# Spreading layer-1 products over the blocks of a GATv2/GCN kernel, and a new order for its end

## Chip, core, metric

The kernel runs on one core of a Trainium2 chip. The metric is device microseconds of one execution; runs are compared by their median.

## What is computed

Two graph layers over 3327 nodes (padded to 3328 = 26 blocks of 128) with 128 features and a sparse adjacency matrix (about 2% of the entries are not zero). Layer 0 is a four-head GATv2, layer 1 a normalised graph convolution. Both are pre-norm with a residual:

```python
h = jnp.maximum(_layernorm(x, axis=-1), 0.0)
# layer 0, for each head
x1 = h @ w1; x2 = h @ w2
E = leaky_relu(x1[:, None, :] + x2[None, :, :], 0.01)
s = jnp.exp(jnp.tanh((E @ a) / 8.0) * 8.0) * adj
s = s / jnp.sum(s, axis=-1, keepdims=True)
out_h = leaky_relu(s @ h @ Wlin.T, 0.01)
x = x + concat(out_h) @ w
# layer 1
h = jnp.maximum(_layernorm(x, axis=-1), 0.0)
A_t = adj + I;  D = A_t.sum(axis=1);  A_norm = D**-0.5 * A_t * D**-0.5
x = x + relu(A_norm @ (h @ W.T + b))
```

## The kernel before

**Layer 0, block by block.** A block is 128 rows of the adjacency matrix. For each block the kernel finds the columns of the non-zero entries, builds lists of row numbers from them, and fetches those rows of two feature tables in DRAM with indirect DMAs that POOL issues (`gather`, line 562). A block has two halves; a half has four windows of 8 gathers (tile `g`, four buffers) and an overflow window of 3 (tile `ge`, one buffer): 70 gathers a block, 1820 in all. TensorE turns the rows (`stage_z`, L587), DVE applies the maximum with the block's own term (L599), TensorE sums to scores (`stage_r`, L610), `finish` makes weights of them and sums the weighted rows (`ag`, L658 and L676), and `close` completes the block: it writes the new x to DRAM (`xn_d`), and leaves in `x_sb[:, b]` the normalised, projected and scaled row block that layer 1 multiplies (L749). A block whose `x_sb` is final is called closed.

**Order.** The schedule is written out by hand. A score group is a slot pair; `slot()` advances everything that runs beside the groups: the closing chains (`tails`), the chains of `finish` (`ends`), the preparation of coming blocks (`advance`, 72 steps a block, some 108 slots a block), and the gathers that fit. Each engine runs its own instructions in this order.

**Preparation** (`prep(b)`) runs a block or more ahead. It turns the 26 column tiles of the block with TensorE, copies them to SBUF tiles `at` (pool `pat`, 3 buffers) with ACT, and writes them to DRAM (`AT_d`, from ACT's queue). `AT_d` holds the transposed matrix by strips: strip s is the four blocks 4s to 4s+3 (the seventh strip has two), so `AT_d` tile (s, j) is 128x512. Then come the list steps: `hTb` is loaded (L424), ACT sums the rows (L426), the next block's `adjb` is loaded (L342, SP's queue, one buffer), the sorted lists are made, and the indices (L450).

**Layer 1** is, for each strip s, a sum over j of `x_sb[:, j]` times tile (s, j), 26 x 7 products, most 128x512. They are made in several places:

- in preparation, from the `at` tiles still in SBUF, for the columns j below `finished(b)` = 4*(b//4) - 2: `known_step` (L370), summed in `part1`, stored to `part1_d` (72 tile columns of a strip in all).
- in the last block and a half, when preparation is over: `begin` (L873), for strips 1 to 3, twelve columns each from `finished(4s)`; tiles come in pairs from `AT_d` to the room of `adjb`, the sum goes to `part2_d`.
- at the end: `layer1` (L937), 74 products. Tiles come 11 at a time into the `g` buffers (`strip`, L847, SP's and ACT's queues). The work begins with strips 0 and 1 without the last column (36 products, one in each slot while the last block's chain runs), then goes strip by strip. `strip_in` loads x, `part1` and, for strips 1 to 3, `part2` (SP's queue, L892 to L896) into two pairs of buffers `r0`, `r1`. `strip_out` adds them, turns the result, scales it, applies relu and the residual and writes the output (L917, ACT's queue).

The half of a table that depends on the adjacency matrix is rewritten for each half block (`weights`, L572, SP's queue).

Of the kernel before, what the change touches and what calls it, by code (L numbers as in the profile page):

```python
# [15 lines left out]
P = 128  # L16
# [3 lines left out]
BANK = 512  # L20
# [44 lines left out]
COLS = 709  # L65
FEAT = 64
# [162 lines left out]
def _sparse_layers(tc, nc, x, adj, w1, w2, a, wlin, w, gw, gb, gb_sb, gwT, x_sb, dinv, flag, ident, out):  # L229
# [24 lines left out]
    with ExitStack() as l0:  # L254
# [26 lines left out]
        pat = l0.enter_context(tc.tile_pool(name="pat", bufs=3))  # L281
# [62 lines left out]
        def prep(b, k):  # L344
# [21 lines left out]
            def known_step(j0, js, at):  # L366
                assert all(blks[j0 + q].closed for q in js)
                pq = bank()
                for q in js:
                    nc.tensor.matmul(pq[:, :P], x_sb[:, j0 + q, :], at[:, q, :], start=(q == 0), stop=(q == js[-1]))  # L370
                yield
                if j0 == 0:
                    k.part1 = pb.tile([P, P], F32, name="part1")
                    nc.scalar.copy(k.part1, pq[:, :P])
                else:
                    nc.vector.tensor_add(k.part1, k.part1, pq[:, :P])
                if j0 + len(js) == finished(b):
                    nc.sync.dma_start(part1_d[:, b * P:(b + 1) * P], k.part1)
# [47 lines left out]
            nc.scalar.activation(adjb, adjb, AF.Copy, accum_out=deg)  # L426
            if 0 < b < NB - 1:
                load(b + 1)
# [23 lines left out]
            k.idx = idx  # L452
            yield
            flat = cand[:, :, :SOME]
# [92 lines left out]
        def rows_in():  # L547
            state["turn"] += 1
            return pgs[state["turn"] % 4].tile([P, WT, ROW], F32, name="g")

        def gather(b, hb, w):

            k = blks[b]
            tab = tables[hb].rearrange("r (c u) -> (r c) u", u=1)
            if w == NW:
                g, n, at = pe_.tile([P, OVT, ROW], F32, name="ge"), OVT, k.idxo[:, hb]
            else:
                g, n, at = rows_in(), WT, k.idx[:, w, WT * hb:WT * hb + WT]

            def one(t):  # L560
                lo = 16 * (t // 2) if w < NW else 0
                return nc.gpsimd.indirect_dma_start(out=g[:, t, lo:COLS], out_offset=None, in_=tab,  # L562
                                                    in_offset=bass.IndirectOffsetOnAxis(ap=at[:, t:t + 1], axis=0))

            queue.extend((k, hb, w, partial(one, t)) for t in range(n))
            k.g[hb, w] = g
# [47 lines left out]
        def finish(k, hb, w):  # L614
# [4 lines left out]
            if w < NW:  # L619
                wq = pb.tile([P, WT, 8], F32, name="wq")  # L620
                diag = bass.AP(g.tensor, g.offset, [list(g.ap[0]), [ROW + 8, 8], [1, 8]])
                nc.vector.tensor_tensor(wq, diag, qmask[:, None, :].to_broadcast([P, WT, 8]), OP.mult)
# [203 lines left out]
        BEGUN = 12  # L826
        strips = {}
        early = {s: range(finished(4 * s), finished(4 * s) + BEGUN) for s in (1, 2, 3) if finished(4 * s) + BEGUN < NB - 3}
# [22 lines left out]
        def begin():  # L851
# [17 lines left out]
            for i, (s, j) in enumerate(work):  # L869
                assert blks[j].closed  # L870
                if j == early[s][0]:
                    po = bank()
                nc.tensor.matmul(po, x_sb[:, j, :], thirds[:, i // PAIR % 3, i % PAIR], start=(j == early[s][0]), stop=(j == early[s][-1]))  # L873
                if i % PAIR == PAIR - 1:
                    bring(i // PAIR + 3)
                if j == early[s][-1]:
                    part2 = pv.tile([P, H, P], F32, name="outT").rearrange("p h i -> p (h i)")
                    nc.scalar.copy(part2, po)
                    nc.sync.dma_start(part2_d[:, 4 * s * P:4 * s * P + BANK], part2)
# [3 lines left out]
        def first_column(s):  # L883
            return early[s][-1] + 1 if s in early else finished(4 * s)

        def strip_in(s):
# [8 lines left out]
            if s in early:  # L895
                nc.sync.dma_start(r0[:, 1], part2_d[:, rows].rearrange("p (b i) -> p b i", b=n))  # L896
            return n, rows, r0, r1

        def strip_out(s, po, n, rows, r0, r1):
# [3 lines left out]
            if s in early:  # L903
                nc.vector.tensor_add(ot, po, ot)
            if finished(4 * s):
                nc.vector.tensor_add(ot, ot if s in early else po, r1[:, 0])
            elif s not in early:
# [12 lines left out]
        front = range(min(2, NS - 1))  # L920
        work = [(s, j) for s in front for j in range(first_column(s), NB - 1)]
        in_front = len(work)
        work += [(s, NB - 1) for s in front] + [(s, j) for s in range(len(front), NS) for j in range(first_column(s), NB)]
        pieces = [work[i:i + PIECE] for i in range(0, len(work), PIECE)]

        def layer1():
            ending, sums, ins = [], {}, {}
            for i, (s, j) in enumerate(work):
# [3 lines left out]
                if s not in sums:  # L932
                    sums[s] = ps_z.tile([P, 2, BANK], F32, name="z")[:, 0]
                if j == min(NB - 1, first_column(s) + 4 * (s not in front)):
                    assert len(ending) < 2
                    ins[s] = strip_in(s)
                nc.tensor.matmul(sums[s][:, :w], x_sb[:, j, :], strips[s, j][:, :w], start=(j == first_column(s)), stop=(j == NB - 1))  # L937
                if i % PIECE == PIECE - 1 or i == len(work) - 1:
                    allow("g")
                ending[:] = [f for f in ending if next(f, "end") != "end"]  # L940
                if j == NB - 1:
                    ending.append(strip_out(s, sums.pop(s), *ins.pop(s)))
                yield "one"
# [7 lines left out]
        with tc.tile_pool(name="pre", bufs=1) as pre, ExitStack() as images:  # L951

            lent = pe_.tile([P, OVT, ROW], F32, name="ge").rearrange("p t c -> p (t c)")[:, :16 * P]
# [353 lines left out]
```

## Time and profile before

| | |
|---|---|
| median of 3 runs | 3246.03 us (3227.53 to 3260.07) |
| the profiled execution | 2536.74 us; its span 2534.9 us, granted TensorE clock 0.98 |
| PE, DVE, POOL, ACT busy | 2278.9, 2030.5, 1791.8, 704.1 us |
| DMA | 838.58 MB, 331 GB/s over the span |
| of it: POOL's queue (gathers) | 640.34 MB |
| SP's queue, ACT's queue | 140.96 MB, 53.88 MB |
| HBM | 765.93 MB read, 113.42 MB written |

The profile is of one execution, which was shorter than the runs of the median; nothing in it says why. "Busy" counts an engine's instructions, not its waits; PE's ends are modelled. A row of windows gives a stretch in us, its length, the busy time (and number of instructions) of PE, its weight loads (PEld), DVE, ACT and POOL, then the granted clock, the share of time in which DMA engines had packets, and GB/s. A row of the timeline gives start, duration, engine, line, operation, tiles and, in brackets, the idle time before and what ended it. A row of waits gives who waited for whom: us in total, times, the longest.

### The profile page before, as it was taken

What the parts mean: (1) busy time and instruction counts of PE and PEld (TensorE: products, weight loads), DVE (VectorE), ACT (ScalarE), POOL (GpSimd) and SP (SyncE); (2) the same over time, 40 slices, a digit from 0 to 9 for tenths busy, and PEclk for the clock granted to TensorE, in tenths of its full rate; (3) what the DMA queues carried; (4) which work ended last, traced back from release to release, by engine and by line L of the source; (5) the groups of instructions that cost most, each with busy time, mean ns of one, the idle gap of its engine ahead of it and who ended that gap; (6) DMA issues with size and microseconds to landing.
All of it is one profiled execution on the core that took longest, in us unless ns stands there. A gap on an engine that the chain in (4) does not pass through costs nothing.

```text
span 2534.9 us, 51974 instructions
## 1 busy us (share of the span) xinstructions
PE 2278.9 (90%) x19410; PEld 1586.2 (63%) x19410; DVE 2030.5 (80%) x6260; ACT 704.1 (28%) x1651; POOL 1791.8 (71%) x1873
## 2 busy tenths in 40 slices
PE   6689899988989998989998999999999899999898
PEld 4456666656666666666666666666666667675553
DVE  7678988888788888878888788988988888895433
ACT  4122233223223222322322322232232233222110
POOL 3577777777777777777777777777777777777620
PEclk9789999999999999999999999999999999999999
DMA  9999999999999999999999999999999999999995
GB/s 294 392 338 314 342 353 318 334 351 335 324 339 346 318 328 359 329 319 343 337 312 336 353 311 341 352 329 329 339 346 318 330 360 313 333 322 347 324 336 186
DMA packets 460759, 838.58 MB, mean 331 GB/s; under 512 B 209099, under 2 KB 318165, under 8 KB 457173
## 3 DMA queue, kind: packets, MB, share of 16 engines
q0 software_dynamic: 145600, 640.34, 71.0%
q1 hardware_dynamic: 219396, 140.96, 19.1%
q10 hardware_dynamic: 95504, 53.88, 7.0%
q8 instruction: 156, 2.56, 0.4%
q14 instruction: 103, 0.84, 0.1%
HBM read 765.93 MB, written 113.42 MB: 347 GB/s over the span
## 4 chain that ended last, share of the span: by engine, by line
PE 35%; DVE 24%; DMA 20%; POOL 11%; issue 7%; ACT 1%; SPq 0%; DVEq 0%; POOLq 0%; ACTq 0%
DMA g<-table,idx 13%; DVE r L599 11%; POOL g L562 10%; PE z L587 10%; PE s L610 6%; PE z L590 3%; DMA ge<-table,idxo 3%; PE z L937 2%; DVE cand L405 2%; PE tr L627 2%; PE ag L658 2%; DMA AT_d<-at 2%; PE tr L370 2%; PE tr L505 1%; DVE codes L401 1%
## 5 line engine op out<-in xcount | busy, mean ns | idle before, releaser
L562 POOL DMA_INDIRECT g<-table,idx x1664 | 1616.3, 971 | 568.3 <-issue 442.2
L599 DVE TENSOR_TENSOR r<-z,x1n 128x1024 f32<-128x1024 f32 x832 | 1010.1, 1215 | 65.5 <-PE z L587 63.9
L587 PE MATMUL z<-ident,g 128*128 128x128 f32 x6656 | 922.4, 278 | 151.9 <-DVE r L599 111.7
L587 PEld LDWEIGHTS z<-ident,g 128*128 128x128 f32 x6656 | 743.8, 142 | 366.9 <-DVE r L599 224.2
L610 PE MATMUL s<-r,sel 128*32 128x512 f32 (+1 forms) x3744 | 491.1, 597 | 0.7 <-ACT ssb L618 0.7
L618 ACT COPY ssb<-s 128x512 f32<-128x512 f32 x260 | 146.7, 564 | 524.6 <-PE s L610 522.5
L630 DVE TENSOR_TENSOR sc<-tr,g 128x32 f32<-128x32 f32 x208 | 38.5, 185 | 300.5 <-PE tr L627 300.5
L405 DVE MAX8 cand<-codes 128x8 f32<-128x52 uint16 x1664 | 215.3, 205 | 0.0
L562 POOL DMA_INDIRECT ge<-table,idxo x156 | 152.6, 978 | 47.5 <-issue 38.1
L638 ACT ACTIVATE th<-sc 128x32 f32<-128x32 f32 x260 | 58.3, 224 | 420.9 <-DVE sc L633 418.5
L590 PE MATMUL z<-oi,x1b 128*128 128x384 f32 x416 | 174.1, 501 | 0.0
L658 PEld LDWEIGHTS ag<-g,wt 128*32 128x32 f32 x3328 | 99.0, 110 | 115.3 <-issue 100.8
L357 ACT COPY at<-tr 128x512 f32<-128x512 f32 (+1 forms) x175 | 97.0, 554 | 222.2 <-PE tr L355 198.3
L627 PE MATMUL tr<-ident,ssb 128*128 128x128 f32 x988 | 153.1, 276 | 5.0 <-ACT ssb L618 4.5
L610 PEld LDWEIGHTS s<-r,sel 128*32 128x32 f32 x3744 | 73.9, 108 | 110.5 <-issue 86.4
L587 PEld LDWEIGHTS z<-ident,ge 128*128 128x128 f32 x624 | 81.4, 146 | 94.8 <-issue 28.5
L596 ACT ACTIVATE r<-z 128x768 f32<-128x768 f32 x104 | 84.3, 810 | 201.7 <-PE z L590 201.7
L658 PE MATMUL ag<-g,wt 128*32 128x133 f32 x3328 | 133.4, 278 | 0.0
L587 PE MATMUL z<-ident,ge 128*128 128x128 f32 x624 | 111.7, 283 | 21.1 <-DMA ge<-table,idxo 18.5
L627 PEld LDWEIGHTS tr<-ident,ssb 128*128 128x128 f32 x988 | 114.3, 141 | 15.3 <-ACT ssb L618 14.9
L355 PE MATMUL tr<-ident,adjb 128*128 128x128 f32 x676 | 107.4, 282 | 16.3 <-DMA adjb<-in_adj_dram 10.2
L401 DVE SCALAR_TENSOR_TENSOR codes<-adjb,code 128x832 uint16<-128x832 f32 x104 | 102.3, 1020 | 1.9 <-DMA adjb<-in_adj_dram 1.9
(188 smaller groups left out, 2350.4 us busy)
## 6 DMA issues: line engine op xcount, KB each, us to landing
adjb<-in_adj_dram SPq DMA_DIRECT2D x26, 1664.0 KB
table<-AT_d SPq DMA_DIRECT2D x52, 832.0 KB
AT_d<-at ACTq DMA_DIRECT2D x150, 256.0 KB
g<-table,idx POOLq DMA_INDIRECT x1664
table<-img SPq DMA_DIRECT2D x12, 1312.0 KB
adjb<-AT_d SPq DMA_DIRECT2D x18, 512.0 KB
g<-AT_d SPq DMA_DIRECT2D x7, 1024.0 KB
g<-AT_d ACTq DMA_DIRECT2D x5, 1024.0 KB
```

Source lines behind the costliest of these rows:

```text
L355: nc.tensor.transpose(pt[:, q, :], adjb[:, (j0 + q) * P:(j0 + q + 1) * P], ident)
L357: nc.scalar.copy(at[:, :n, :], pt[:, :n, :])
L401: nc.vector.scalar_tensor_tensor(codes[:, i], adjb[:, c0:c0 + part], 0.0, code[:, c0:c0 + part], op0=OP.not_equal, op1=OP.mult, accum_out= ...
L405: nc.vector.max(cand[:, c, 8:].rearrange("p (r s) -> p r s", s=32)[:, :, sgm % 32], codes.rearrange("p a b -> p (a b)")[:, sgm % 32 * SEG: ...
L562: return nc.gpsimd.indirect_dma_start(out=g[:, t, lo:COLS], out_offset=None, in_=tab, in_offset=bass.IndirectOffsetOnAxis(ap=at[:, t:t + 1 ...
L587: nc.tensor.matmul(z[:, i, q * P:(q + 1) * P], g[:, m % 2 * 4 + q, PROJ + h * D:PROJ + (h + 1) * D], ident, is_transpose=True, start=(q == ...
L590: nc.tensor.matmul(z[:, i, :n], k.x1b[:, h * D:(h + 1) * D], k.oi[:, hb * n:(hb + 1) * n], start=False, stop=True, skip_group_check=True)
L599: nc.vector.tensor_tensor(r.rearrange("p h (i s) -> p h i s", s=16), z.rearrange("p h (i s) -> p h i s", s=16), k.x1n[:, 2 * hp:2 * hp + 2 ...
L610: nc.tensor.matmul(k.s[32 * h:32 * h + 32, :n], sel[:, h, 31 - at:63 - at], rs[h // 2][:, h % 2, :n], start=(at == 0), stop=(at == 1 or m ...
L618: nc.scalar.copy(ssb[:, :nk * P], s[:, :nk * P])
L627: nc.tensor.transpose(pt[:, q, :], ssb[:, q * P:(q + 1) * P], ident)
L658: nc.tensor.matmul(ag[32 * cg:32 * cg + 32, u, :WORK], wt[:, t].rearrange("p h q -> p (h q)"), g[:, t, FEAT:FEAT + WORK], start=(w == 0 an ...
```

## The change

Preparation of block b may now take a run of three products of layer 1 (`part_of`). It picks the closed strip with the most columns that are ready (block closed, two behind) and not yet summed, loads three `AT_d` tiles from DRAM into the `at` buffers, and, if the strip has a sum already, that too (`part2_d`). The loads are issued after ACT's row sum and ahead of the next `adjb`; the six matmuls stand behind the index step; the sum is added (or copied, the first time) a step later and stored. `pat` has 4 buffers instead of 3; `part1` has one instead of two, and rows of `g` and `ge` are 712 wide instead of 720.

`begin` now takes four columns each of strips 0 to 5, from where the runs ended, and adds to the stored sum where there is one. `first_column` follows. In the end, the order is: strips 0 to 3 without the last column (12 products, in the slots of the last chain), then the last columns two at a time between the remaining strips: 29 products. Two strips share a double PSUM tile, and `strip_in` looks five products ahead.

```diff
+WIDE = 712
-        pat = l0.enter_context(tc.tile_pool(name="pat", bufs=3))
+        pat = l0.enter_context(tc.tile_pool(name="pat", bufs=4))
...
-                    k.part1 = pb.tile([P, P], F32, name="part1")
+                    k.part1 = pb.tile([P, P], F32, name="part1", bufs=1)
...
             nc.scalar.activation(adjb, adjb, AF.Copy, accum_out=deg)
+            mine = part_of(b)
+            next(mine)
             if 0 < b < NB - 1:
                 load(b + 1)
...
             k.idx = idx
-            yield
+            next(mine, None)
+            yield
+            next(mine, None)
...
-            return pgs[state["turn"] % 4].tile([P, WT, ROW], F32, name="g")
+            return pgs[state["turn"] % 4].tile([P, WT, WIDE], F32, name="g")
...
-                g, n, at = pe_.tile([P, OVT, ROW], F32, name="ge"), OVT, k.idxo[:, hb]
+                g, n, at = pe_.tile([P, OVT, WIDE], F32, name="ge"), OVT, k.idxo[:, hb]
...
-        BEGUN = 12
+        BEGUN = 4
+        RUN = 3
         strips = {}
-        early = {s: range(finished(4 * s), finished(4 * s) + BEGUN) for s in (1, 2, 3) if finished(4 * s) + BEGUN < NB - 3}
+        runs, known = {}, [finished(4 * s) for s in range(NS)]
+        for b in range(NB):
+            s = max(range(max(1, (b + 1) // 4)), key=lambda s: b - 2 - known[s])
+            if b >= 3 and b - 2 - known[s] >= RUN:
+                runs[b] = s, known[s]
+                known[s] += RUN
+        early = {s: range(known[s], known[s] + BEGUN) for s in range(NS - 1) if NB > 12 and known[s] + BEGUN < NB - 2}
+        begun = {s for s, _ in runs.values()}
+
+        def part_of(b):
+
+            if b not in runs:
+                yield
+                return
+            s, j0 = runs[b]
+            wide = AT_d[s * NP + j0 * P:s * NP + (j0 + RUN) * P, :].rearrange("(j p) i -> p j i", p=P)
+            cols = [pat.tile([P, 4, P], F32, name="at").rearrange("p a b -> p (a b)") for _ in range(RUN)]
+            for q in range(RUN):
+                nc.sync.dma_start(cols[q], wide[:, q])
+            total = pat.tile([P, 4, P], F32, name="at").rearrange("p a b -> p (a b)")
+            place = part2_d[:, 4 * s * P:4 * s * P + BANK]
+            if j0 > finished(4 * s):
+                nc.sync.dma_start(total, place)
+            yield
+            pq = bank()
+            for q in range(RUN):
+                assert blks[j0 + q].closed
+                nc.tensor.matmul(pq, x_sb[:, j0 + q, :], cols[q], start=(q == 0), stop=(q == RUN - 1))
+            yield
+            if j0 > finished(4 * s):
+                nc.vector.tensor_add(total, total, pq)
+            else:
+                nc.scalar.copy(total, pq)
+            nc.sync.dma_start(place, total)
...
+                place = part2_d[:, 4 * s * P:4 * s * P + BANK]
                 if j == early[s][0]:
                     po = bank()
+                    part2 = pat.tile([P, 4, P], F32, name="at").rearrange("p a b -> p (a b)")
+                    if s in begun:
+                        nc.sync.dma_start(part2, place)
...
                 if j == early[s][-1]:
-                    part2 = pv.tile([P, H, P], F32, name="outT").rearrange("p h i -> p (h i)")
-                    nc.scalar.copy(part2, po)
-                    nc.sync.dma_start(part2_d[:, 4 * s * P:4 * s * P + BANK], part2)
+                    if s in begun:
+                        nc.vector.tensor_add(part2, part2, po)
+                    else:
+                        nc.scalar.copy(part2, po)
+                    nc.sync.dma_start(place, part2)
...
-            return early[s][-1] + 1 if s in early else finished(4 * s)
+            return early[s][-1] + 1 if s in early else known[s]
...
-            if s in early:
+            if s in early or s in begun:
                 nc.sync.dma_start(r0[:, 1], part2_d[:, rows].rearrange("p (b i) -> p b i", b=n))
...
-        front = range(min(2, NS - 1))
-        work = [(s, j) for s in front for j in range(first_column(s), NB - 1)]
-        in_front = len(work)
-        work += [(s, NB - 1) for s in front] + [(s, j) for s in range(len(front), NS) for j in range(first_column(s), NB)]
+        left = [[(s, j) for j in range(first_column(s), NB)] for s in range(NS)]
+        if NS > 6:
+            rest, last = [part[:-1] for part in left], [part[-1:] for part in left]
+            order = rest[:4] + last[:2] + rest[4:5] + last[2:4] + rest[5:6] + last[4:6] + left[6:]
+            in_front = sum(map(len, rest[:4]))
+        else:
+            order, in_front = left, len(left[0]) - 1
+        work = [w for part in order for w in part]
...
                 if s not in sums:
-                    sums[s] = ps_z.tile([P, 2, BANK], F32, name="z")[:, 0]
-                if j == min(NB - 1, first_column(s) + 4 * (s not in front)):
-                    assert len(ending) < 2
-                    ins[s] = strip_in(s)
+                    if not banks:
+                        two = ps_z.tile([P, 2, BANK], F32, name="z")
+                        banks += [two[:, 0], two[:, 1]]
+                    sums[s] = banks.pop(0)
...
+                if i >= in_front - 1:
+                    for s1, j1 in work[i:i + 5]:
+                        if j1 == NB - 1 and s1 not in ins and s1 not in gone and len(ins) + len(ending) < 2 and (i >= in_front or s1 < NS - 3 or s1 == 0):
+                            ins[s1] = strip_in(s1)
                 ending[:] = [f for f in ending if next(f, "end") != "end"]
                 if j == NB - 1:
+                    if s not in ins:
+                        bring(s)
+                    gone.add(s)
                     ending.append(strip_out(s, sums.pop(s), *ins.pop(s)))
+                    next(ending[-1])
```

More of the change, by code (lines that the diff above doesn't have):

```diff
@@ L620, in finish @@
                 wq = pb.tile([P, WT, 8], F32, name="wq")
-                diag = bass.AP(g.tensor, g.offset, [list(g.ap[0]), [ROW + 8, 8], [1, 8]])
+                diag = bass.AP(g.tensor, g.offset, [list(g.ap[0]), [WIDE + 8, 8], [1, 8]])
                 nc.vector.tensor_tensor(wq, diag, qmask[:, None, :].to_broadcast([P, WT, 8]), OP.mult)
@@ L902, in strip_out @@
             po = po[:, :n * P].rearrange("p (b i) -> p b i", b=n)
-            if s in early:
+            more = s in early or s in begun
+            if more:
                 nc.vector.tensor_add(ot, po, ot)
             if finished(4 * s):
-                nc.vector.tensor_add(ot, ot if s in early else po, r1[:, 0])
-            elif s not in early:
+                nc.vector.tensor_add(ot, ot if more else po, r1[:, 0])
+            elif not more:
                 nc.scalar.copy(ot, po)
@@ L917, in strip_out, with bring @@
             nc.scalar.dma_start(out[rows, :].rearrange("(b p) d -> p b d", p=P), xo)
-        front = range(min(2, NS - 1))
-        work = [(s, j) for s in front for j in range(first_column(s), NB - 1)]
-        in_front = len(work)
-        work += [(s, NB - 1) for s in front] + [(s, j) for s in range(len(front), NS) for j in range(first_column(s), NB)]
+        left = [[(s, j) for j in range(first_column(s), NB)] for s in range(NS)]
[6 more added lines that the diff above has]
+        work = [w for part in order for w in part]
         pieces = [work[i:i + PIECE] for i in range(0, len(work), PIECE)]
         def layer1():
-            ending, sums, ins = [], {}, {}
+            ending, sums, ins, banks, gone = [], {}, {}, [], set()
+            def bring(s):
+                while len(ins) + len(ending) > 1:
+                    ending[:] = [f for f in ending if next(f, "end") != "end"]
+                ins[s] = strip_in(s)
             for i, (s, j) in enumerate(work):
@@ L951, in _sparse_layers @@
         with tc.tile_pool(name="pre", bufs=1) as pre, ExitStack() as images:
-            lent = pe_.tile([P, OVT, ROW], F32, name="ge").rearrange("p t c -> p (t c)")[:, :16 * P]
+            lent = pe_.tile([P, OVT, WIDE], F32, name="ge").rearrange("p t c -> p (t c)")[:, :16 * P]
             blks[0].at = list(lent.rearrange("p (i k c) -> p i k c", i=4, k=4)[:, i] for i in range(4))
```

## Prediction

> **What bounds the kernel now.** I read the page first: PE 90% busy, DVE 80%, POOL 71%, DMA engines near 9 in every slice. Busy shares don't say who sets the pace, so I went on to POOL's timeline inside the loop, where it only issues row gathers, and to windows of the gathers alone.
>
> ```profile
> L562 POOL DMA_INDIRECT g<-table,idx x1664 | 1616.3, 971 | 568.3 <-issue 442.2
> ...
> 1485.20 0.94 POOL L562 DMA_INDIRECT g<-table,idx  x1 [0.30 <-issue]
> 1486.45 0.95 POOL L562 DMA_INDIRECT g<-table,idx  x1 [0.30 <-issue]
> 1487.70 0.95 POOL L562 DMA_INDIRECT g<-table,idx  x1 [0.30 <-issue]
> ...
> 170.00:2427.00 2257.00, 1700.14 (x1751) 0.99 0.99 334
> ```
>
> Each gather takes 0.95 us and the next begins 0.30 us later with nothing awaited: one per 1.25 us. In 170 to 2427 us, 1751 gathers in 2257 us are 1.29 us each; a block has 70 of them, so 90 us. The 29% by which POOL looks idle is mostly this 0.30 us (1751 x 0.30 = 525 of 557 us). POOL's wait for a buffer that PE has still to read is small, the third row below. So in the loop POOL sets the pace. How near PE comes is read from windows of six blocks (548 to 1087) and four late ones (1540 to 1894), and from what PE waited for in the latter:
>
> ```profile
> 548.00:1087.00 539.00, 486.44 (x4346) 342.67 (x4347) 454.88 (x1404) 156.74 (x372) 409.72 (x421) 1.00 0.99 335
> 1540.00:1894.00 354.00, 330.45 (x2998) 237.47 (x2992) 306.02 (x946) 105.16 (x249) 269.13 (x277) 1.00 0.99 336
> ...
> POOL g L562 <- PE ag L658: 16.4, 7, 5.5
> ...
> PE z L587 <- DVE r L599: 15.3, 18, 1.6
> ```
>
> First columns: window length, PE busy. Early PE is idle 52.6 us in six blocks (8.8 a block) and partly waits for gathers (10.1 us of such waits in that window). Late it is idle 23.6 us in four (5.9 a block), and there its waits name DVE, not a gather. PE is then a close second to POOL.
>
> After the last gather (2427 us) comes the end, which has no POOL work:
>
> ```profile
> 2446.00:2485.00 39.00, 38.30 (x160) 18.76 (x152) 6.70 (x31) 5.55 (x16) 0.00 (x0) 1.00 0.93 331
> 2485.00:2535.00 50.00, 37.88 (x105) 18.13 (x104) 19.45 (x31) 0.77 (x2) 0.00 (x0) 0.89 0.42 133
> ...
> 2445.10 0.81 PE L590 MATMUL z<-oi,x1b 128*128 128x384 f32 x2
> 2450.52 7.89 PE L937 MATMUL z<-g,x_sb 128*128 128x512 f32 x18
> 2484.78 0.40 ACT L749 ACTIVATE x_sb<-agn,dinv 128x128 f32<-128x128 f32 x1 [4.58 <-DMA r<-xn_d]
> 2491.67 38.23 ACTq L917 DMA_DIRECT2D out_dram<-r  x7
> 2494.13 0.37 SPq L892 DMA_DIRECT2D r<-xn_d  x1
> 2499.33 0.69 DVE L904 TENSOR_TENSOR r<-z,r 128x512 f32<-128x512 f32 x1 [5.64 <-DMA r<-part_d]
> ```
>
> The last score matmul ends at 2445.9, the last row block of x is final at 2485.2, all ends at 2534.9. A layer-1 product is two matmuls, 18 of which take 7.89 us: 0.86 us a product, and 74 of them fill these 89 us.
>
> **Skill.** "DMA: Bandwidth & Descriptors", section "SWDGE vs HWDGE vs iDMA", says that GpSimd builds the descriptors of its DMAs in software. The even 1.25 us without a wait agrees, and the forecast goes by the 1.25. "TensorE: Matmul & The Clock Gate", part 1, says that a PE left idle falls to a slower clock. The granted clock of 0.89 in the last window agrees mildly; I price the end at that, not at half.
>
> **The change, part by part.** Written out from the loops: 19 blocks of preparation (5, 7, 8, 10 to 25) get a run of three products, 57 in all, for strips 0 to 4. The early part goes from 36 products (strips 1 to 3) to 24 (four for each of strips 0 to 5). 110 - 57 - 24 = 29 stay for the end instead of 74.
>
> *PE in the loop.* A run is 6 matmuls x 0.43 = 2.6 us; 19 runs are 49 us. Bounds: 0 if idle time covers them, 49 if none does. Runs of blocks 5 to 14 (8) fall where PE waits for gathers and has 8.8 us idle: 0. The 11 later ones fall where PE is idle 5.9 us, but mostly in hand-overs with DVE; I take it that 1.6 of the 2.6 us are absorbed and 1.0 isn't: 11 us.
>
> *DVE and ACT.* 14 adds of 128x512 from PSUM (0.69 us, as L904) and 5 copies (0.59, as L878): 13 us over 19 blocks in which DVE is idle 12 to 14 us each. 0. If DVE's slack were gone, 13. The add waits for PE, and DVE's next r operations stand behind it for at most the run's 2.6 us; PE in turn waits for those r, which is in the 1.0 above.
>
> *SP and DMA.* 57 column loads, 14 loads and 19 stores of a sum, 256 KB each: some 0.4 us of issue apiece on SP, which is mostly waiting. They stand ahead of the next adjb load. The first load of a sum waits for the last AT_d write from the same rotating buffer; behind it wait adjb (then needed a third of a block later or more) and the half-table write (issued 36 us before its first gather at 1442.9: gather at 1478.8). A few microseconds fit: 0. New bytes: 33 sums here, 5 loads and 3 more stores early, 3 loads in the end, 44 x 0.26 = 11.5 MB of 838.6. At 335 GB/s that is 34 us were DMA the bound, against 45 tiles (12 MB) that leave the end. While adjb loads (1431 to 1446 us) DMA moved 408 GB/s, in a quiet stretch (1366 to 1392) 287; so there is room, and I take 0. The run's matmuls come 20 preparation steps (some 25 us) after the loads. POOL's queue gets nothing; rows of 712 for 720 only change a stride: 0, bound either way by nothing the trace shows.
>
> *Early part.* 12 products fewer: 10 us of PE in the last block, where PE lags: the last gathers are issued by 2427.3, z ends 18 us later. About 8 of these come back; 0 if other work holds it, 10 at most. SP carries 12 pair loads for 18, plus 5 sum loads.
>
> *The closing chain* of block 25, 2445.9 to 2485.2 = 39.3 us, now stands in PE's queue among 36 products (72 matmuls of L937 in that window), one per slot. After, 12 go in front and then nothing. Its own operations, as long as this trace shows them, with hand-overs: about 10 us to the last ag, 13 from there to x_sb; plus the overlap with 12 products, about 29. Gain 10 (bounds 4 and 14).
>
> *From x_sb to the end*, 49.7 us now, carries 38 products (77 matmuls, 35 us). After: 17 products (15 us), but seven strips through two pairs of buffers. A pair of strips needs: output landed before the next load (2491.67 to 2494.13: 2.5 us), load (2494.13 to 2499.33: 5.2), DVE 5 x 0.69 for each. That is 12 us a pair: first pair done at 8, two more pairs 24, the short last strip 7, the final write and check 5.4: 44.5. Three more 0.69 adds are inside. Gain 5 (bounds -5 and 14).
>
> Sum on the profiled execution: +11 - 8 - 10 - 5 = -12 us of 2536.7 (span 2534.9), -0.5%. The median shown is 3246.03, 1.28 times as long, and no view says what was slower there. I carry the share over: 3246 x 0.995 = 3230. The gap matters for the cases: if those runs had a slower PE, PE would be the bound and rival 1 gains weight; if POOL's issue was slower, PE had slack and rival 2 does.
>
> **Rivals.**
> 1. *PE becomes the bound in the loop.* Place: the run between score groups; price 2.6 us x 19 = 49. Against it the gains of 23: +26 us, +1.0%, 3279. It decides as soon as idle hand-overs with DVE don't shrink, and would show as POOL waiting for ag. For it: the late window's 93% with no gather waits. Against: early blocks do wait for gathers.
> 2. *The loop pays nothing, the end gives all* its bounds: -10 - 14 - 14 = -38, with some of it lost -33: -1.3%, 3204. For it: POOL's unbroken cadence.
> 3. *Bursts.* 1.3 MB ahead of adjb's 1.7 MB delays gathers. At the 120 GB/s between 408 and the quiet 287 the extra needs some 10 us to drain; if 3 us of that reach PE in 19 blocks, +57 - 23 = +34, +1.3%, 3290. For it: DMA share 0.99. Against: PE's small gather waits now.
> That the change doesn't do what it says is no case: the counts follow from its loops.
>
> **Chances.** Forecast 0.45, rival 1 0.20, rival 2 0.22, rival 3 0.13. The predicted time is the forecast's, 3230; its own range 3195 to 3260. The runs before lie within 1.0% of each other, which is about what a measurement of this kernel can tell from no change. 8 in 10 takes in rivals 2 and 1 and part of 3: 3170 to 3300. Faster by over 1%: most of rival 2 and a part of the forecast, 0.30; within 1%: 0.42, the rest of the forecast and a part of rival 1; slower by over 1%: 0.28, from rivals 1 and 3.
>
> **What would show it.** POOL's rate in 170 to 2427 stays 1.29 us a gather (forecast) or goes over 1.31 with ag waits (rival 1) or with PE waiting for g (rival 3); the last score matmul ends sooner after the last gather; x_sb's last write comes 29 us after it, not 39; about 44 us follow. It is wrong if the last strips queue for buffers longer than 12 us a pair, or if SP's order makes a half-table late.

## The result: slower by 0.9%, and the profile after

| | before | after |
|---|---|---|
| median, the same chip | 3236.56 us (19 runs) | 3268.01 us (19 runs) |
| ratio after / before | | 1.0087, 95% interval 1.0064 to 1.011 |
| profiled execution | 2536.74 us, clock 0.98 | 3254.88 us, clock 0.917 |

28 us were lost where 16 were to be won. The ratio is of the fast runs alone, without the one of the 19 after that was slow; that of the two medians is 1.0097. The time, 3268, lies in the range of 8 in 10 (3170 to 3300) and not in the forecast's own (3195 to 3260), and the sign was wrong. And the two profiles are not of one kind: that of before is of an execution of 2537 us, that of after is like the timed runs. So the first thing needed was a profile of the kernel *before* at the time that was timed. The unchanged kernel, run again on another chip (e1_before), gave it (3304.07 us, clock 0.916).

First the page's row for the gathers, then the window of POOL alone over the loop (busy time, clock, DMA share, GB/s), and POOL's waits, of the changed kernel:

```profile
L567 POOL DMA_INDIRECT g<-table,idx x1664 | 1626.8, 978 | 1183.2 <-PE ag L663 560.5
```
```profile
170.00:3152.00 2982.00, 1717.95 (x1763) 0.93 0.83 262
```
```profile
POOL g L567 <- PE ag L663: 560.5, 178, 13.9
POOL g L567 <- issue: 430.6, 1389, 3.9
```

A gather is as long as in the prediction's profile (978 against 971 ns). But 1763 of them now take 2982 us, 1.69 us each instead of 1.29, and POOL waits 178 times, 560 us in all, for a buffer that PE's `ag` products still read. In the prediction's profile that wait was 16.4 us. POOL does not set the pace here. Nor did the change make it so; the same rows of the unchanged kernel in its run of 3304 us:

```profile
L562 POOL DMA_INDIRECT g<-table,idx x1664 | 1625.2, 977 | 1204.3 <-PE ag L658 640.9
```
```profile
170.00:3188.00 3018.00, 1719.42 (x1763) 0.92 0.81 251
```

What makes PE late is not more work: both executions of the kernel before have 19410 matmuls, though PE is busy 2609.2 us in the longer one and 2278.9 in the shorter. Three rows of the page, first from the execution of 2537 us and then from that of 3304 us (busy us, mean ns, then PE's idle time just before and what ended it):

```profile
L587 PE MATMUL z<-ident,g 128*128 128x128 f32 x6656 | 922.4, 278 | 151.9 <-DVE r L599 111.7
...
L627 PE MATMUL tr<-ident,ssb 128*128 128x128 f32 x988 | 153.1, 276 | 5.0 <-ACT ssb L618 4.5
...
L658 PE MATMUL ag<-g,wt 128*32 128x133 f32 x3328 | 133.4, 278 | 0.0
```
```profile
L587 PE MATMUL z<-ident,g 128*128 128x128 f32 x6656 | 1027.3, 299 | 297.3 <-DVE r L599 171.7
...
L627 PE MATMUL tr<-ident,ssb 128*128 128x128 f32 x988 | 182.5, 312 | 133.9 <-issue 76.0
...
L658 PE MATMUL ag<-g,wt 128*32 128x133 f32 x3328 | 201.4, 281 | 89.1 <-issue 87.3
```

"Issue" is idle time in which PE waited for nothing that the profile shows. The execution of 2537 us has next to none of it at PE's matmuls (1.6 us). Below, PE's timeline of the run of 3304 us at one group of 16 `ag` products, which in the execution of 2537 us takes 0.64 us without a gap:

```profile
1993.86 0.53 PE L658 MATMUL ag<-g,wt 128*32 128x133 f32 x9
1994.82 0.42 PE L658 MATMUL ag<-g,wt 128*32 128x133 f32 x3 [0.44 <-issue]
1995.54 0.30 PE L658 MATMUL ag<-g,wt 128*32 128x133 f32 x1 [0.30 <-issue]
1996.94 0.42 PE L658 MATMUL ag<-g,wt 128*32 128x133 f32 x3 [1.10 <-issue]
```

The group takes 3.5 us here. Of the 208 groups 46% take over 1 us and 24% over 2 us; in the execution of 2537 us none takes more than 0.84. The clock is not what slows this group: in its stretch, below, the granted clock was 1.00 (the third number from the end), as it was all through 89 of the 96 groups of over 1 us.

```profile
1993.80:1997.40 3.60, 1.72 (x20) 0.73 (x12) 0.43 (x1) 0.00 (x0) 1.75 (x2) 1.00 0.98 391
```

This slowness goes with the chip, or with its state at that time; no chip was met twice. Over the comparisons the kernel before took 3236.6, 3304.0, 3232.6 and 3239.3 us on four chips and 2534.0 and 2534.3 us on two, in every run on each. They are called slow and quick chips from here. The profile that the prediction read was like those of a quick chip, and its time was measured on a slow one.

The end does not depend on that. Windows of the changed kernel from the last score matmul to the last write of `x_sb`, and on to the last instruction:

```profile
3172.00:3199.00 27.00, 20.57 (x112) 11.18 (x108) 6.70 (x31) 5.38 (x16) 0.00 (x0) 0.88 0.39 131
3199.00:3253.00 54.00, 26.26 (x62) 12.49 (x62) 21.62 (x34) 0.28 (x1) 0.00 (x0) 0.69 0.32 97
```

39 us became 27, and 50 became 54, though PE has only 62 matmul records left in the last one where it had 105. The timeline of the second stretch (out goes the first strip of a pair, in come the next rows, they are added, the next pair's output is ready, its rows come in) says what it waits for:

```profile
3210.19 37.78 ACTq L963 DMA_DIRECT2D out_dram<-r  x7
3212.64 0.37 SPq L937 DMA_DIRECT2D r<-xn_d  x1
...
3217.71 0.69 DVE L950 TENSOR_TENSOR r<-z,r 128x512 f32<-128x512 f32 x1 [5.26 <-DMA r<-part_d]
...
3220.57 0.69 DVE L950 TENSOR_TENSOR r<-z,r 128x512 f32<-128x512 f32 x1 [1.44 <-PE z L993]
...
3223.13 0.69 DVE L960 TENSOR_TENSOR r<-tr,x_sb 128x512 f32<-128x512 f32 x1 [1.14 <-PE tr L959]
...
3224.58 0.69 DVE L962 SCALAR_TENSOR_TENSOR r<-r,r 128x512 f32<-128x512 f32 x1
...
3227.73 0.37 SPq L937 DMA_DIRECT2D r<-xn_d  x1
```

From load to load of a buffer pair: 15.1 us. Of these, 5.1 pass from the load to the first addition, and 7.6 from there to the first strip's last operation, in which DVE does its five operations for that strip and two for the other, and waits for PE twice. 2.45 us pass from the issue of an output to the load that may overwrite its buffer. The Trainium skill, "DMA: Bandwidth & Descriptors", section "Anatomy of one DMA — SWDGE (gpsimd) path", gives a DMA that GpSimd issues a fixed cost of some 2 us, most of it the confirmation that its last byte has landed. The 2.45 us are near that, but here ACT's queue issued the output, and what they are made of no run shows.

### The profile page after: what moved, and what is told of

It reads as the page before. It is cut to its first block, busy times and chain, and to the rows that moved or that the text cites. A ratio compares the mean times of both kernels' runs of the same rounds, so it can differ in the third digit from the quotient of the medians.

```text
span 3253.0 us, 52243 instructions
## 1 busy us (share of the span) xinstructions
PE 2549.0 (78%) x19410; PEld 1746.0 (54%) x19410; DVE 2065.0 (63%) x6282; ACT 690.8 (21%) x1653; POOL 1798.1 (55%) x1873
## 4 chain that ended last, share of the span: by engine, by line
PE 51%; DVE 19%; another core or an unknown queue 13%; issue 7%; ACT 5%; DMA 3%; POOL 1%; ACTq 0%; DVEq 0%; SPq 0%; POOLq 0%
PE z L592 17%; DVE r L604 9%; PE s L615 9%; PE z L595 4%; PE tr L632 4%; ACT r L601 2%; DVE cand L406 2%; PE ag L663 2%; PE tr L371 2%; PE tr L356 2%; PE tr L861 2%; DMA g<-table,idx 1%; POOL g L567 1%; PE ag L681 1%
## 5 line engine op out<-in xcount | busy, mean ns | idle before, releaser
L592 PE MATMUL z<-ident,g 128*128 128x128 f32 x6656 | 1018.3, 297 | 320.2 <-DVE r L604 193.0
L592 PEld LDWEIGHTS z<-ident,g 128*128 128x128 f32 x6656 | 827.2, 153 | 556.8 <-DVE r L604 284.5
L615 PE MATMUL s<-r,sel 128*32 128x512 f32 (+1 forms) x3744 | 529.0, 612 | 8.6 <-issue 7.1
L632 PE MATMUL tr<-ident,ssb 128*128 128x128 f32 x988 | 177.2, 305 | 122.4 <-ACT ssb L623 74.8
L663 PE MATMUL ag<-g,wt 128*32 128x133 f32 x3328 | 200.7, 281 | 85.3 <-issue 82.6
L663 PEld LDWEIGHTS ag<-g,wt 128*32 128x32 f32 x3328 | 123.0, 110 | 239.1 <-issue 230.1
L632 PEld LDWEIGHTS tr<-ident,ssb 128*128 128x128 f32 x988 | 124.5, 155 | 154.7 <-ACT ssb L623 101.2
L371 PE MATMUL tr<-at,x_sb 128*128 128x128 f32 x488 | 79.9, 308 | 90.0 <-ACT at L358 64.6
L371 PEld LDWEIGHTS tr<-at,x_sb 128*128 128x128 f32 x488 | 66.4, 209 | 114.2 <-ACT at L358 83.5
```

The costliest lines, as they stand in the source:

```text
L592: nc.tensor.matmul(z[:, i, q * P:(q + 1) * P], g[:, m % 2 * 4 + q, PROJ + h * D:PROJ + (h + 1) * D], ident, is_transpose=True, start=(q == ...
L615: nc.tensor.matmul(k.s[32 * h:32 * h + 32, :n], sel[:, h, 31 - at:63 - at], rs[h // 2][:, h % 2, :n], start=(at == 0), stop=(at == 1 or m ...
L632: nc.tensor.transpose(pt[:, q, :], ssb[:, q * P:(q + 1) * P], ident)
L663: nc.tensor.matmul(ag[32 * cg:32 * cg + 32, u, :WORK], wt[:, t].rearrange("p h q -> p (h q)"), g[:, t, FEAT:FEAT + WORK], start=(w == 0 an ...
```

## The experiments

**How they are read.** Ratios are to the kernel before on the same chip. To see the loop alone (first to last gather), the tail is taken off: loop difference = (ratio - 1) x median before, less the difference of the tails after the last gather. The tail is that of the one profiled execution; it was 114.2 us for the kernel before on a slow chip and 107.6 on a quick one, and repeats to about 3 us (104.2 in e8, which has the same end). The +/- is half the ratio's interval; it holds neither these 3 us nor what may differ between two slow chips. Runs of one chip are e1 to e4, e14 to e17, and e18 with e19; e5, e6, e8 and e9, and e10 to e13.

| run | what stays of the change | chip | ratio, 95% interval | tail, us | loop difference, us |
|---|---|---|---|---|---|
| e1_before | nothing | slow | 1.0002 (0.9978, 1.0026) | 114.2 | +1 +/- 8 |
| e2_order | end's order, widths, buffers | slow | 1.0019 (0.9999, 1.004) | 121.3 | -1 +/- 7 |
| e3_runs | all but the end's order | slow | 1.0042 (1.0021, 1.0062) | 87.3 | +41 +/- 7 |
| e4_loads | all but the 57 products and the additions | slow | 0.9972 (0.9952, 0.9993) | 103.7 | +1 +/- 7 |
| after | all | slow | 1.0087 (1.0064, 1.011) | 100.5 | +42 +/- 7 |
| e14_products | bare products | slow | 1.0029 (1.0013, 1.0044) | 101.6 | +22 +/- 5 |
| e17_columns | products, column loads | slow | 1.001 (0.999, 1.0031) | 99.4 | +18 +/- 7 |
| e18_adds | products, additions | slow | 0.9985 (0.9963, 1.0007) | 99.8 | +10 +/- 7 |
| e19_moves | products, all transfers | slow | 1.0055 (1.0028, 1.0082) | 103.8 | +28 +/- 9 |
| e15_twice | all, products twice | slow | 1.029 (1.0256, 1.0324) | 101.2 | +107 +/- 11 |
| e16_both | before, no early products, third row pair | slow | 1.004 (1.0022, 1.0058) | 134.9 | -8 +/- 6 |
| e5_products | bare products | quick | 0.9956 (0.9942, 0.997) | 94.1 | +2 +/- 4 |
| e11_products | bare products | quick | 0.9971 (0.9961, 0.998) | 94.3 | +6 +/- 3 |
| e10_after | all | quick | 1.0039 (1.0025, 1.0054) | 93.5 | +24 +/- 4 |
| e6_twice | all, products twice | quick | 1.0167 (1.0141, 1.0193) | 92.8 | +57 +/- 7 |
| e12_twice | all, products twice | quick | 1.0186 (1.0166, 1.0205) | 93.4 | +61 +/- 5 |
| e9_none | before, no early products | quick | 1.005 (1.0032, 1.0068) | 126.1 | -6 +/- 5 |
| e13_third | before, third row pair | quick | 0.9989 (0.9976, 1.0002) | 101.5 | +3 +/- 3 |
| e8_tiny | before, 2808 small ACT copies | quick | 0.9991 (0.9979, 1.0004) | 104.2 | +1 +/- 3 |

**The change taken apart, on a slow chip.** e1_before is the kernel before once more. e2_order keeps the new end and switches the runs off; e3_runs does the reverse; e4_loads keeps the loads, reads and stores of the runs but not their products.

> The kernel before, unchanged, to see the timed executions from inside. Theory 1 (in the executions that are timed PE sets the pace, not POOL): the median is within 0.3% of 3237 us, the profile is about as long, a block takes 117 to 119 us instead of 90, POOL waits for ag for over 400 us in all, the granted clock is near 0.92. Theory 2 (POOL sets the pace and only issues more slowly): the step of the gathers is 1.6 us throughout, and PE waits for gathers.

> Only the new order of the end, with its pools and widths; no runs, the early part as before (12 columns of strips 1 to 3), 74 products at the end. Theory 1 (the runs cost PE time in the loop): no change, 3225 to 3245 us. Theory 2 (the end's order costs: seven strips through two pairs of buffers): slower by 10 to 25 us, 3247 to 3262.

```diff
-            if b >= 3 and b - 2 - known[s] >= RUN:
+            if False:
```

> The runs and the early part of the change, with the end's order of before (strips 0 and 1 first, then strip by strip). Theory 1: the loss stays, 3260 to 3275 us. Theory 2: most of the loss is gone, 3230 to 3245.

```diff
-            order = rest[:4] + last[:2] + rest[4:5] + last[2:4] + rest[5:6] + last[4:6] + left[6:]
...
+        front = range(min(2, NS - 1))
+        work = [(s, j) for s in front for j in range(first_column(s), NB - 1)]
+        work += [(s, NB - 1) for s in front] + [(s, j) for s in range(len(front), NS) for j in range(first_column(s), NB)]
```

> The change without the 57 products and the sums of the runs: their column loads, sum loads and stores stay (what is stored is not a sum), so the 57 products are left out of the result. Theory 1 (PE time, 57 x 0.86 = 49 us at full clock, more at 0.92): 45 to 65 us below the changed kernel, 3203 to 3223. Theory 3 (loads, stores and SP's order cost it): less than 15 us below it, over 3253.

```diff
-            pq = bank()
-            for q in range(RUN):
-                nc.tensor.matmul(pq, x_sb[:, j0 + q, :], cols[q], start=(q == 0), stop=(q == RUN - 1))
...
-                nc.vector.tensor_add(total, total, pq)
+            nc.sync.dma_start(place, cols[0] if j0 == finished(4 * s) else total)
```

The loop pays 41 us as soon as the runs are in (e3), and 1 +/- 7 when only their transfers are (e4). So on this chip the products with their additions cost some 40 us +/- 10, and what the transfers do to SP's order nothing that is seen, as long as no product waits for them. The end's order alone costs 7 us (121.3 against 114.2): with the runs in, the old order has a tail of 87.3 us and the new one of 100.5. What the end gained, it gained by having fewer products.

This chip's kernel before took 3304 us and not the 3237 of these texts, so only ratios compare. By them e2 agrees with its theory 1 (at most 1.0025). e3 lies between its theories (from 1.007, and up to 1.0025), since the old order gives back 13 us of tail. e4 excludes theory 3 (over 1.005) and stays just above theory 1 (0.990 to 0.996).

**Products alone, and twice.** e5_products takes `w1_sb`, which is on the chip, for the products' second operand, without loads and sums; e6_twice repeats the three products of each run.

> The changed kernel whose 57 products stay in the preparations but take a tile that is already on the chip as their second operand; the column tiles are not loaded, and the sums are neither added nor stored nor read at the end. So the output lacks the true values of these products. Theory PE (a product costs its own PE time, about 0.8 us, in the loop of the timed executions): nothing is gained by the missing loads, adds and stores, and the ratio to the kernel before lies at 1.006 to 1.010, as for the whole change (1.0087); the loop, first to last gather, is 40 to 46 us longer than in the kernel before at the same clock. Rival DMA and queues (the 171 column loads, 51 reads and 57 writes of 256 KB, or their place on SP's queue, set the loss): the ratio falls to 0.995 to 1.000, that of the change without products or below.

```diff
-        begun = {s for s, _ in runs.values()}
+        begun = set()
...
-                nc.tensor.matmul(pq, x_sb[:, j0 + q, :], cols[q], start=(q == 0), stop=(q == RUN - 1))
+                nc.tensor.matmul(pq, x_sb[:, j0 + q, :], w1_sb.rearrange("p h d -> p (h d)"), start=(q == 0), stop=(q == RUN - 1))
```

(The counts in that text are some three times too high: 19 runs load 57 columns and 14 sums and store 19.)

> The changed kernel in which each run makes its three products twice in a row into the same bank (the second set restarts the sum), so 57 products more on PE, with no load, wait or other instruction added. Theory PE: the 57 cost 38 to 49 us once more (0.67 to 0.86 us each), so the ratio to the kernel before goes from 1.0087 to 1.020 to 1.024. Rival (the loss comes from what surrounds the runs: waits for column tiles, buffers, order of the preparation): PE has room for bare products, at most 15 us are added, and the ratio stays under 1.014.

```diff
-            for q in range(RUN):
+            for q in range(2 * RUN):
-                nc.tensor.matmul(pq, x_sb[:, j0 + q, :], cols[q], start=(q == 0), stop=(q == RUN - 1))
+                nc.tensor.matmul(pq, x_sb[:, j0 + q % RUN, :], cols[q % RUN], start=(q % RUN == 0), stop=(q % RUN == RUN - 1))
```

> The kernel before with one ScalarE copy of one element per partition added in every slot of the main loop (2808 instructions more on ACT, for which nobody waits). Theory PE (matmul time is the bound, and an instruction on another engine costs PE nothing): within 0.5% of the kernel before, at most +15 us. Rival (what limits PE in the timed executions is a supply or a recording of instructions that all engines share): 2808 instructions are about 7% more than there are, and the time grows by more than 60 us, 1.9% or more.

```diff
+            nc.scalar.copy(tiny, tiny)
```

(2808 is 5% of the 51974 instructions that the trace has, not 7%.)

> The kernel before without its 36 early products in the last blocks: all of layer 1's products are made at the end. Theory PE bound up to the last gather: a product in the loop costs about 0.79 us (45 us over 57), at the end 0.47 us (the 57 products fewer took 27 us off the tail), so the 36 give 28 us back and cost 17: 11 us faster, ratio 0.9965, 0.994 to 0.999. Rival (in the last blocks PE has slack, so the early products are free there): the end grows by 17 us and nothing comes back, ratio 1.004 to 1.007.

```diff
-        early = {s: range(finished(4 * s), finished(4 * s) + BEGUN) for s in (1, 2, 3) if finished(4 * s) + BEGUN < NB - 3}
+        early = {}
```

(There the end's products that went with the 27 us are 45, 74 less 29; the other 12 were early ones.)

These four met a quick chip, for which their numbers had not been written. The ratio of e5 that would have spoken for "DMA and queues" is no verdict on the slow chips, nor is e6's 1.0167, which lies between its theories. e8 excludes a common limit of issued instructions only for a quick chip. e9 comes out as its rival said: without the 36 early products, which stand in the last block and a half, when preparation is over, the loop is only 6 us +/- 5 shorter, and the tail 18 us longer.

**The same on further chips, told apart by the time of the kernel before.**

> The changed kernel itself, on a further chip. So far the kernel before took 3304 us on one chip and 2534 us on another, and the changed kernel was timed only where it took 3237 us. Theory (POOL sets the pace where PE is quick, PE where it is slow): where the kernel before takes about 2534 us, the loop hides most of the 57 products and the end's gain remains, ratio 0.994 to 0.999; where it takes 3240 to 3300 us, 1.006 to 1.011. Rival (the loss belongs to the change on any chip): 1.006 to 1.011 in both.

> The run without column loads, sums and stores once more (its output lacks the true values of the 57 products; ratio 0.9956 on the chip of 2534 us). Theory: where the kernel before takes 3240 to 3300 us, bare products cost their PE time, ratio 1.006 to 1.010; on a chip of 2534 us again 0.994 to 0.997. Rival (loads, sums and stores make the loss where PE is slow): 0.995 to 1.000 in both.

> The run with each product made twice once more (1.0167 on the chip of 2534 us). Theory: where the kernel before takes 3240 to 3300 us, 38 to 49 us more than the changed kernel beside it, ratio 1.020 to 1.024; on a chip of 2534 us the second 57 products no longer find room under POOL and cost 0.8 us each, so the changed kernel beside it is 35 to 50 us faster. Rival (something else than PE time): under 1.014 on a slow chip, and less than 20 us from the changed kernel on a quick one.

This was a quick chip again. The changed kernel loses there too, 0.39%; the theory's 0.994 to 0.999 fell, and the rival's 1.006 to 1.011 as well. But what costs there is something else. Loop windows of bare products (e11), of the whole change (e10) and of doubled products (e12), POOL alone:

```profile
170.00:2428.00 2258.00, 1702.83 (x1751) 1.00 0.99 333
```
```profile
170.00:2440.00 2270.00, 1706.36 (x1751) 1.00 1.00 343
```
```profile
170.00:2481.00 2311.00, 1706.87 (x1751) 1.00 0.99 337
```

Before, it was 2257 us for the same 1751 gathers: 57 bare products are hidden under POOL's cadence. The loads, sums and stores then cost 18 us +/- 4 (24 less 6). DMA engines had packets for 0.99 of the time already; windows of 400 to 1200 and 1200 to 2000 us (the last two columns are DMA's share and GB/s) of e11 and of e10:

```profile
400.00:1200.00 800.00, 731.87 (x6418) 510.24 (x6416) 669.02 (x2064) 232.04 (x548) 606.89 (x622) 1.00 0.99 334
1200.00:2000.00 800.00, 752.64 (x6626) 533.25 (x6625) 675.48 (x2095) 234.21 (x550) 605.12 (x623) 1.00 0.99 334
```
```profile
400.00:1200.00 800.00, 732.66 (x6437) 512.47 (x6439) 673.24 (x2075) 234.53 (x551) 607.20 (x620) 1.00 1.00 344
1200.00:2000.00 800.00, 747.26 (x6608) 529.93 (x6608) 677.33 (x2097) 235.01 (x551) 604.65 (x619) 1.00 1.00 345
```

The extra 25 MB find 10 GB/s more, and the share goes to 1.00. At 334 GB/s they would have filled 75 us; the loop grew by 18, so a share of 0.99 was not yet the limit. That fits the prediction's third rival, at a third of its price (18 us of 57); but e10 has the additions too, for which DVE waits (14 times, 23.2 us in all), and no run split the two on a quick chip. Doubling the products costs 37 us +/- 6 more, 0.65 us a product, as e12's text expected (35 to 50): now PE's slack is used up, and POOL's waits in e12 say so (22.8 us in e10).

```profile
POOL g L567 <- PE ag L663: 72.9, 67, 10.0
```

> The kernel before with a third pair of row tiles at its end (in the tile that held the adjacency rows), so that the rows of strip s come in when strip s-3 has left and not strip s-2. Theory (the rest of the end is a cycle of two pairs, some 12 to 15 us for each two strips): the stretch from the last write of x_sb to the end falls from 48 to 50 us to 38 to 43, ratio 0.996 to 0.998. Rival (what the last strips wait for is their products or the transfers themselves): under 3 us of it, ratio 0.999 to 1.001.

```diff
-            r0 = pr.tile([P, 2, BANK], F32, name="r0").rearrange("p k (b d) -> p k b d", b=4)[:, :, :n]
-            r1 = pr.tile([P, 2, BANK], F32, name="r1").rearrange("p k (b d) -> p k b d", b=4)[:, :, :n]
+            if s % 3 < 2:
+                two = [pr.tile([P, 2, BANK], F32, name=name) for name in ("r0", "r1")]
+            else:
...
+                two = [state["third"][:, t] for t in range(2)]
+            r0, r1 = (t.rearrange("p k (b d) -> p k b d", b=4)[:, :, :n] for t in two)
```

Windows of e13's end, cut as the prediction cut the kernel before:

```profile
2445.00:2484.00 39.00, 38.29 (x161) 18.91 (x160) 6.70 (x31) 5.40 (x15) 0.00 (x0) 1.00 0.91 327
2484.00:2528.00 44.00, 35.20 (x106) 16.82 (x104) 19.45 (x31) 0.99 (x2) 0.00 (x0) 0.95 0.48 152
```

The last stretch is 44 us for 50, but in e8, whose end is that of the kernel before, it was 46; the ratio's interval holds 1. PE is busy 35 of the 44 us: in the kernel before the products themselves, not the buffers, fill most of the end. The ratio, 0.9989, lies with the rival (0.999 to 1.001), though the interval does not exclude the theory's 0.998. The version is not shown to be faster, and no other version that computes the whole output was.

**Back on slow chips.** The bare and the doubled products once more, e9's and e13's edits together, and three runs that split what is left.

> The runs' bare products once more, without column loads, sums and stores (the output lacks their true values): 0.9956 and 0.9971 on two chips where the kernel before takes 2534 us. Where it takes 3240 to 3300 us: theory PE (each of the 57 products costs 0.7 to 0.8 us of the loop there, and the end gives 14 us back) 1.005 to 1.010; rival (the loss there comes from loads, sums and stores) 0.994 to 0.999. Where it takes 2534 us: 0.995 to 0.998 again.

> The changed kernel with each of the 57 products made twice: 1.0167 and 1.0186 where the kernel before takes 2534 us (the changed kernel beside the second 1.0039). Where it takes 3240 to 3300 us: theory PE 38 to 49 us above the changed kernel, 1.019 to 1.024; rival under 1.014. Where it takes 2534 us: 1.016 to 1.020.

> The kernel before without its 36 early products and with the third pair of row tiles at the end. Where the kernel before takes 3240 to 3300 us: theory PE (a product costs 0.7 to 0.8 us in the loop, 0.47 at the end) gains 11 us from the first edit and 4 from the second, 0.993 to 0.998, a kernel quicker than both; rival (the early products are free in the last blocks) 1.002 to 1.006. Where it takes 2534 us the first edit alone gave 1.005 and the second 0.9989: 1.002 to 1.006.

> The changed kernel whose runs load their column tiles and make their products, but whose sums are neither read nor added nor stored (the output lacks these products); it tells apart the 57 column loads from the 19 stores and their reads. Where the kernel before takes 2534 us, the loads, sums and stores together cost 16 us (1.0039 less 0.9971 is 0.7%): if by their bytes (57 column tiles of some 82 that move), this run keeps two thirds of it, 1.001 to 1.003; if by the sums' own waits, it falls to that of bare products, 0.996 to 0.998. Where it takes 3240 to 3300 us, they cost at most 6 us, and the run stays within 0.3% of the run of bare products beside it.

(As in e5, the end does not read the sums of the runs.)

```diff
-            total = pat.tile([P, 4, P], F32, name="at").rearrange("p a b -> p (a b)")
-                nc.sync.dma_start(total, place)
...
-                nc.vector.tensor_add(total, total, pq)
-            nc.sync.dma_start(place, total)
```

> The runs' products and the reading of their bank (an addition on DVE or a copy on ACT, 19 in all) without any transfer: no column loads, no sums read or stored, the end does not add them (the output lacks them). On slow chips bare products left the loop 25 us longer than in the kernel before, products with column loads 26, the whole change 45. Theory (the 19 additions make the other 20 us: each holds DVE and a bank that PE needs): where the kernel before takes 3230 to 3300 us, ratio 1.006 to 1.010. Rival (the sums' transfers make it): 1.001 to 1.004, that of bare products. Where it takes 2534 us, by the same token 1.001 to 1.004 against 0.995 to 0.998.

(That text reckons the loop from medians, 25, 26 and 45 us; from the ratios, as in the table, it is 22, 18 and 42. `held` is `w1_sb`, which is on the chip and stands in for the columns too.)

```diff
-                nc.vector.tensor_add(total, total, pq)
+                nc.vector.tensor_add(total, held, pq)
-            nc.sync.dma_start(place, total)
```

> The counterpart: the whole change, products, column loads, reads and stores, but with no addition: what is stored is a tile that was loaded, so the output lacks these products, and nobody reads the products' bank. Theory additions: where the kernel before takes 3230 to 3300 us, ratio 1.000 to 1.004; where it takes 2534 us, 0.995 to 0.999. Rival transfers: 1.006 to 1.010 on a slow chip, 1.002 to 1.005 on a quick one.

```diff
-                nc.vector.tensor_add(total, total, pq)
-            nc.sync.dma_start(place, total)
+            nc.sync.dma_start(place, cols[0] if j0 == finished(4 * s) else total)
```

Where a quick chip's loop hid the bare products, a slow chip's pays 22 us +/- 5 (e14, whose ratio lies between its two theories). Doubled, they cost 65 +/- 13 more than the change on its own chip (e15, above both its theories), 1.1 us each, where a run of three occupies PE for 2.74 us, 0.91 a product:

```profile
2953.30 2.74 PE L861 MATMUL tr<-at,x_sb 128*128 128x512 f32 x6
```

So a slow chip charges for products, also with nothing else added. But the sum does not close. Bare products 22 and transfers alone 1 make 23, not 42. e17 clears the column loads: 18 +/- 7 beside e14's 22 on the same chip. e18, which has the additions and no transfers, has 10 +/- 7 and lies under both its theories. e19, transfers with the products, has 28 +/- 9 and lies between its theories, with an interval that reaches into both. The rest, some 15 to 20 us, appears only in the two runs with all parts together (e3 and the change itself), and the intervals are too wide to give it to one of them. Besides, no slow chip ran both the whole change and bare products. e18 does more than e14 and yet has 12 us less, on another chip, so part of the gap may be a difference between chips. e16 came out as its rival said: without the 36 early products the loop is 8 us +/- 6 shorter, so they are nearly free on a slow chip as well.

## Why the prediction was wrong

- **"I carry the share over: 3246 x 0.995 = 3230."** This is the main step that failed. The sum was made on an execution in which POOL sets the pace, and carried to runs 1.28 times as long without asking who sets it there. The text had the fork ("if those runs had a slower PE, PE would be the bound and rival 1 gains weight") and gave rival 1 a chance of 0.20. Such runs were what was timed: POOL waits 641 us for PE in the kernel before, where the profile that was read had 16.
- **"PE in the loop ... 11 us."** On the chips of its profile this was enough, if anything too high: 2 and 6 us for bare products. Where it was timed the runs cost 42, near rival 1's 49. That rival 1's +26 us came so near the measured +28 is in part luck: the loop cost 7 us less than it said, and the end gave 14 us net, not 23. Of the 42, products with their additions make 40 +/- 10 on one chip (e3 less e4), and bare products 22 +/- 5 on another; how it divides stays open.
- **"SP and DMA ... I take 0", "DVE and ACT ... 0."** On slow chips the transfers alone cost 1 +/- 7 us (e4). On quick ones transfers and additions cost 18 us: the room read from two short stretches, 408 and 287 GB/s, was too little over the loop, whose share was 0.99. Hence the forecast failed on the profile's own kind of chip as well: 24 - 4 - 13 + 3 = +10 us, +0.39%, not -0.5%.
- **"Early part ... 8."** The lag after the last gather shrank from 26.6 to 19.5 us (slow) and from 18.6 to 14.3 (quick): right on the one, half on the other.
- **"The closing chain ... about 29. Gain 10."** Right: 27.3 and 26.5 us, a gain of 12 to 13. It is not owed to the new order: with the old one (e3) the chain took 23.1.
- **"12 us a pair ... Gain 5."** Mis-sized: a pair took 15.1 us, as the timeline above shows. The prediction's own parts, with DVE's five operations for both strips, add up to 14.6 (2.5 + 5.2 + 6.9), not 12; over the two pairs that alone takes away the gain of 5. The stretch became 5 us longer on a slow chip and 3 on a quick one. The prediction had named a queue of over 12 us a pair as a sign of being wrong.

On the slow chips: 42 - 7 - 12 + 5 = 28 us. The -12 us of the forecast missed by the loop's term for 31 us and by the last stretch for 10.

## What to carry to other kernels

When the profiled execution and the timed runs differ by a quarter, the profile's bound is not the timed runs' bound: price each edit for both and give the chances by which of them will be timed. Work moved out of an end and into a loop was nearly free here where another engine set the loop's pace, and was not where its own engine held the others up; making the moved work alone, and then twice, tells the two cases apart. A DMA share of 0.99 was neither the limit nor a sign of free room. At an end with few products left, the turn-round of buffers (output landed, rows in, additions) was the price of a strip, and the new order cost 7 to 13 us.

## What was not expected of the hardware

The same program takes 2534 us on two chips and 3233 to 3304 us on four, at the same counts of instructions and with gathers of the same length (971 and 977 ns). PE starts many instructions late without a shown wait: such idle time of PE's matmuls is 285 us in e1, and 1.6 us in the execution of 2537 us. That is part of the 767 us between the two; the rest is longer matmul records and longer waits between engines, and what causes all this is open.

The clock is at most a part of it. In both traces it is granted either in full or by half: by half for 105 us of the quick execution and for 557 us of the slow one, which makes the means of 0.98 and 0.92. An estimate from these: half of the 452 us more, 226 us at most, could have been lost by it. The Trainium skill, "TensorE: Matmul & The Clock Gate", part 1, has PE fall to a slower clock when it idles, so part of the lower clock may follow from the gaps. The gaps do not follow from the lower clock in the `ag` groups, most of which were slow at full clock.
